# GATv2 and GCN on one core: x1 turned instead of multiplied, and six list rounds on half of the candidates

## The chip, the cores and the metric

The kernel runs on one core of one Trainium2 chip. The metric is the device time in microseconds (us) of one execution; of five executions shown for the kernel before, the median is 2499.34 us. A profiled execution gives the trace from which all durations of single instructions come. Engines are named as the profile names them: PE is TensorE (PEld its weight loads), DVE is VectorE, ACT is ScalarE, POOL is GpSimd, SP is SyncE. All data are float32.

## The reference

Two graph layers work on 3327 nodes (padded to 3328 = 26 blocks of 128) with 128 features. The adjacency matrix is dense in memory but sparse in content: a row has 63 neighbours on the average and at most 96, the node itself not counted.

```
h = relu(layernorm(x))
for each of 4 heads:
    x1, x2 = h @ w1, h @ w2
    s[i, j] = a . leaky_relu(x1[i] + x2[j])          # 128 features
    s = exp(8 tanh(s / 8)) * adj;  s = s / rowsum(s)
    out = leaky_relu(s @ h @ Wlin.T)
x = x + concat(out of the heads) @ w
h = relu(layernorm(x))
x = x + relu(D^-1/2 (adj + I) D^-1/2 (h @ W.T + b))
```

## The kernel before, in words

The kernel computes the first layer's scores only where the adjacency matrix is not zero. For this it makes, for each block of 128 rows (destinations), lists of the neighbours of each row, and gathers the neighbours' rows from a table in DRAM. A row of this table holds h, the linear part of the scores, x2 of the four heads and two stretches of adjacency weights.

A block has two halves of 64 rows, and each half is worked off in nine groups m. Groups 0 to 7 belong to the 64 list slots of each row: a gather brings 128 table rows, 8 destinations with 16 slots each. POOL issues these gathers at L595, 8 to a tile `g`, with four such tiles (`rows_in`). Group 8 is the overflow: rows with more than 64 neighbours put the rest into a shared list of up to 256 entries for each half (`oi`, `ge`, `FOUND` = 2), with up to 40 entries for one row (`EXTRA`). If a row or a half has more, a flag opens a dense path at the end of the program (`_dense_layer0`, `_dense_layer1`).

For each group, `stage_z` transposes the x2 part of the gathered rows on PE into a PSUM tile `z` (L622), two heads at a time; DVE then takes the maximum of z and x1n, which is -x1 with features on the partitions, into `r` (L638). Group 8 has a matmul of its own that adds x1 by rows, `x1b`, through a selection matrix `oi` (L625 and L627), and DVE (L633) and ACT (L635) make `r` from it. `stage_r` multiplies `r` with the attention vector (L657). `finish` takes the scores through tanh and exp and sums the weighted neighbours on PE (L706, L724). `close` finishes the block.

The lists of block b + 1 are made while block b is worked off, by the generator `prep`. At each `yield` it hands back control. `slot()` is called twice for each pair of heads of a group, some 108 times a block, and lets `prep` go on so that its 72 steps (`NPREP`) keep pace; `tails` and `ends`, the later stages of `finish` and `close`, are advanced in the same place. The order of instructions on each engine is fixed by this when the program is built.

The steps of `prep` that matter here are these:

- Rows of the adjacency matrix become codes: 0 for no edge, and otherwise the number of columns minus the column (L410). 64 segments of 52 codes each give their 8 largest with one MAX8 (L422), 32 segments for each half of the columns. The candidates of half c that the list rounds look at stand in `cand[:, c, :SOME]`, 136 values: the four largest of each segment, and the 8 largest of what is left of the half (L425).
- `select(r)` is one list round (L450 to L457): MAX8 takes the 8 largest candidates into the list (L453), and MATCH_REPLACE8 puts zeros in their places (L456). There are 13 rounds, r = 0 to 12; the last has no MATCH_REPLACE8. Rounds 0 to 7 fill the 64 slots, rounds 8 to 12 the 40 entries beyond. Which candidates a round looks at is chosen in L452: in turns one half (136 values) for r < 4, and both halves (`flat`, 272 values) from then on.
- The lists become indices (L463 to L475) and overflow entries (L486 to L547).
- x1 is computed twice from hTb, the block's h with features on the partitions. L551 makes x1 by rows with one matmul of 512 columns; ACT copies it from PSUM into `x1b` (L553). After one `yield`, L557 makes x1 with features on the partitions, with four matmuls of 128 columns, one for each head; ACT writes its negative into `x1n` (L559). Each of the two results has a bank of the PSUM pool `ps_tr`.

## Time and profile before

| | us |
|---|---|
| median of five executions | 2499.34 (2495.57 to 2508.67) |
| profiled execution | 2499.25 |
| its span, first to last instruction | 2497.5 |
| from one block's L551 to the next (671.07 to 758.63) | 87.6 |
| PE waits (PE and PEld) for DVE's L638, whole run | 114.3 and 171.2 |
| DVE waits for PE's L622 (before L638) and L627 (before L633) | 127.3 and 134.1 |
| ACT's copy into x1b (L553), mean | 0.585 |
| ACT's copy into x1n (L559), mean | 0.597 |

In a line of groups, the columns are: source line, engine, operation, what it writes and reads by the program's names, partitions x elements, count, then busy time in us and the mean of one in ns, and last the idle time of the engine just before these instructions and what ended it. A line of the timeline has the start in us, the duration in us (of a run of like instructions merged), engine, source line, operation and, in brackets, the idle time before it and who ended it. A float32 matmul stands in the profile as two passes, each with a weight load.

### The profile page before, as it was taken

Reading aid. Unit: us, or ns where it says so; the run is one execution under the profiler, and the core shown is the slowest. Engines: PE = TensorE matmul, PEld = TensorE weight load, DVE = VectorE, ACT = ScalarE, POOL = GpSimd, SP = SyncE. Lnnn points to the kernel's source line nnn. Section 1 sums busy time; section 2 is a strip of 40 time slices with the busy share of each in tenths; the row PEclk is TensorE's granted clock in tenths of the full one; section 3 lists DMA queues with packets and bytes.
Section 4 is the critical chain, followed back from the end, with each engine's and each line's share of the span. In section 5 each row is a group of like instructions: output and inputs, shape, how many; then the busy total and the mean of one; then the engine's idle time right before and its main releaser. Section 6 shows DMA issues by size and latency. Waiting matters only on the chain.

```text
span 2497.5 us, 52385 instructions
## 1 busy us (share of the span) xinstructions
PE 2255.3 (90%) x19410; PEld 1596.2 (64%) x19410; DVE 2063.2 (83%) x6426; ACT 680.9 (27%) x1703; POOL 1736.2 (70%) x1822
## 2 busy tenths in 40 slices
PE   6589999989988999999999999999999999999988
PEld 4466666666666666666676666666677666666643
DVE  7688888888898898889888888988988898896623
ACT  4122232223222222322222222232232223222110
POOL 3577777777777777777777777777777777777700
PEclk9699999999999999999999999999999999999989
DMA  9999999999999999999999999999999999999995
GB/s 299 383 337 327 357 326 323 339 349 317 335 366 321 330 351 347 323 331 364 327 327 349 337 314 334 348 321 335 351 332 321 348 352 313 335 327 348 365 273 161
DMA packets 417844, 826.94 MB, mean 331 GB/s; under 512 B 38435, under 2 KB 288815, under 8 KB 414255
## 3 DMA queue, kind: packets, MB, share of 16 engines
q0 software_dynamic: 141440, 619.41, 70.7%
q1 hardware_dynamic: 165343, 147.87, 18.5%
q10 hardware_dynamic: 110800, 56.25, 7.5%
q8 instruction: 156, 2.56, 0.4%
q14 instruction: 105, 0.86, 0.1%
HBM read 754.47 MB, written 113.22 MB: 347 GB/s over the span
## 4 chain that ended last, share of the span: by engine, by line
PE 39%; DVE 26%; DMA 17%; POOL 10%; issue 6%; ACT 1%; SPq 0%; DVEq 0%; ACTq 0%; POOLq 0%
DVE r L638 14%; DMA g<-table,idx 13%; PE z L622 13%; POOL g L595 10%; PE s L657 10%; DVE cand L422 3%; PE ag L706 2%; PE z L627 2%; DVE codes L410 1%; PE z L988 1%; DVE cand L456 1%; DMA g<-AT_d 1%; DVE lists L453 1%; PE tr L675 1%; PE tr L924 1%
## 5 line engine op out<-in xcount | busy, mean ns | idle before, releaser
L595 POOL DMA_INDIRECT g<-table,idx x1664 | 1612.3, 969 | 584.5 <-issue 417.9
L638 DVE TENSOR_TENSOR r<-z,x1n 128x1024 f32<-128x1024 f32 x832 | 1009.8, 1214 | 129.6 <-PE z L622 127.3
L622 PE MATMUL z<-ident,g 128*128 128x128 f32 x6656 | 935.1, 279 | 99.1 <-DVE r L638 88.0
L622 PEld LDWEIGHTS z<-ident,g 128*128 128x128 f32 x6656 | 754.7, 143 | 260.8 <-DVE r L638 137.7
L657 PE MATMUL s<-r,sel 128*2 128x512 f32 (+1 forms) x3744 | 497.5, 584 | 8.3 <-ACT r L635 3.9
L666 ACT COPY ssb<-s 128x512 f32<-128x512 f32 x260 | 146.6, 564 | 500.8 <-PE s L657 500.0
L657 PEld LDWEIGHTS s<-r,sel 128*2 128x2 f32 x3744 | 79.8, 83 | 249.8 <-issue 188.1
L422 DVE MAX8 cand<-codes 128x8 f32<-128x52 uint16 x1664 | 217.1, 204 | 0.0
L686 ACT ACTIVATE th<-sc 128x32 f32<-128x32 f32 x260 | 58.4, 225 | 439.1 <-DVE sc L681 412.9
L706 PEld LDWEIGHTS ag<-g,wt 128*32 128x32 f32 x3328 | 99.9, 110 | 90.2 <-issue 80.5
L367 ACT COPY at<-tr 128x512 f32<-128x512 f32 (+1 forms) x175 | 97.1, 555 | 208.5 <-PE tr L365 195.6
L675 PE MATMUL tr<-ident,ssb 128*128 128x128 f32 x988 | 150.8, 273 | 1.7 <-ACT ssb L666 1.7
L633 DVE TENSOR_TENSOR r<-z,x1n 128x128 f32<-128x128 f32 x104 | 30.0, 288 | 136.7 <-PE z L627 134.1
L706 PE MATMUL ag<-g,wt 128*32 128x133 f32 x3328 | 140.6, 281 | 0.0
L453 DVE MAX8 lists<-cand 128x8 f32<-128x272 f32 (+1 forms) x338 | 133.0, 394 | 2.2
L365 PE MATMUL tr<-ident,adjb 128*128 128x128 f32 x676 | 109.0, 284 | 26.0 <-DMA adjb<-in_adj_dram 15.8
L635 ACT ACTIVATE r<-z 128x512 f32<-128x512 f32 x104 | 62.1, 597 | 246.4 <-DVE r L633 240.3
L627 PE MATMUL z<-oi,x1b 128*128 128x256 f32 x416 | 124.3, 381 | 0.0
L675 PEld LDWEIGHTS tr<-ident,ssb 128*128 128x128 f32 x988 | 118.1, 141 | 8.6 <-ACT ssb L666 2.4
L595 POOL DMA_INDIRECT ge<-table,idxo x104 | 100.8, 969 | 31.7 <-issue 16.8
L456 DVE MATCH_REPLACE8 cand<-lists,cand 128x272 f32<-128x272 f32 (+1 forms) x312 | 117.8, 378 | 0.0
L410 DVE SCALAR_TENSOR_TENSOR codes<-adjb,code 128x832 uint16<-128x832 f32 x104 | 105.2, 1014 | 13.8 <-DMA adjb<-in_adj_dram 13.8
(199 smaller groups left out, 2406.8 us busy)
## 6 DMA issues: line engine op xcount, KB each, us to landing
adjb<-in_adj_dram SPq DMA_DIRECT2D x26, 1664.0 KB
table<-AT_d SPq DMA_DIRECT2D x26, 1664.0 KB
AT_d<-at ACTq DMA_DIRECT2D x150, 256.0 KB
g<-table,idx POOLq DMA_INDIRECT x1664
table<-img SPq DMA_DIRECT2D x12, 1296.0 KB
adjb<-AT_d SPq DMA_DIRECT2D x72, 128.0 KB
g<-AT_d ACTq DMA_DIRECT2D x25, 256.0 KB
g<-AT_d SPq DMA_DIRECT2D x25, 256.0 KB
```

The lines of the kernel that those rows point to most:

```text
L410: nc.vector.scalar_tensor_tensor(codes[:, i], adjb[:, c0:c0 + part], 0.0, code[:, c0:c0 + part], op0=OP.not_equal, op1=OP.mult, accum_out= ...
L422: nc.vector.max(cand[:, c, 8:].rearrange("p (r s) -> p r s", s=32)[:, :, sgm % 32], codes.rearrange("p a b -> p (a b)")[:, sgm % 32 * SEG: ...
L453: nc.vector.max(top, of)
L456: nc.vector.match_replace(out=of, in_to_replace=top, in_values=of, imm_value=0.0)
L595: return nc.gpsimd.indirect_dma_start(out=g[:, t, lo:hi], out_offset=None, in_=tab, in_offset=bass.IndirectOffsetOnAxis(ap=at[:, t:t + 1], ...
L622: nc.tensor.matmul(z[:, i, q * P:(q + 1) * P], g[:, m % 2 * 4 + q, c0:c0 + D], ident, is_transpose=True, start=(q == 0 or m < 8), stop=(m ...
L627: nc.tensor.matmul(z[:, i, :n], k.x1b[:, h * D:(h + 1) * D], k.oi[:, hb * n:(hb + 1) * n], start=False, stop=True, skip_group_check=True)
L638: nc.vector.tensor_tensor(r.rearrange("p h (i s) -> p h i s", s=16), z.rearrange("p h (i s) -> p h i s", s=16), k.x1n[:, 2 * hp:2 * hp + 2 ...
L657: nc.tensor.matmul(k.s[32 * h:32 * h + 2, :n], sel[:, h, 31 - at:33 - at], r[h // 2][:, h % 2, :n], start=(at == 0), stop=(at == 1 or m == 8))
L666: nc.scalar.copy(ssb[:, :nk * P], s[:, :nk * P])
L675: nc.tensor.transpose(pt[:, q, :], ssb[:, q * P:(q + 1) * P], ident)
L706: nc.tensor.matmul(ag[32 * cg:32 * cg + 32, u, :WORK], wt[:, t].rearrange("p h q -> p (h q)"), g[:, t, f0:f0 + WORK], start=(w == 0 and t ...
```

## The change

Two lines of `prep` change. Rounds 4 and 5 of the lists look at one half of the candidates each, as rounds 0 to 3 do, so that of the 64 slots 24 + 24 come from the two halves and 16 from both together. And x1 with features on the partitions is no longer multiplied from w1 and hTb; it is turned on PE from `x1b`, head by head, with `ident` as the other operand. The steps, the yields, the PSUM banks and all other instructions stay.

```diff
             def select(r):
                 top = lists[:, 8 * r:8 * r + 8]
-                of = cand[:, r % 2, :SOME] if r < 4 else flat
+                of = cand[:, r % 2, :SOME] if r < 6 else flat
                 nc.vector.max(top, of)
...
             pm = bank()
             for h in range(H):
-                nc.tensor.matmul(pm[:, h * P:(h + 1) * P], w1_sb[:, h, :], hTb, start=True, stop=True)
+                nc.tensor.transpose(pm[:, h * P:(h + 1) * P], x1b[:, h * P:(h + 1) * P], ident)
```

## Prediction, made before the result was known

> **What bounds the kernel now.** I read the page's busy shares and its chain first.

> ```profile
> PE 2255.3 (90%) x19410; PEld 1596.2 (64%) x19410; DVE 2063.2 (83%) x6426; ACT 680.9 (27%) x1703; POOL 1736.2 (70%) x1822
> PE 39%; DVE 26%; DMA 17%; POOL 10%; issue 6%; ACT 1%; SPq 0%; DVEq 0%; ACTq 0%; POOLq 0%
> ```

> No engine is the bound alone: TensorE (PE) and VectorE (DVE) hand the end to each other inside each block. The waits say so: DVE waits 134.1 us for the matmuls of L627 and 127.3 us for the transposes of L622; PE and its weight loads wait 114.3 and 171.2 us for L638 on DVE. For gathered rows PE waits only 8.0 us. So the question for each edit is which engine is late where it stands. For that I priced both edits by the groups with shapes kept apart (columns: count, busy us, mean ns), and then looked in the timeline at where they fall.

> ```profile
> L453 DVE MAX8 lists<-cand 128x8 f32<-128x272 f32 x234 | 102.6, 439 | 2.2
> L456 DVE MATCH_REPLACE8 cand<-lists,cand 128x272 f32<-128x272 f32 x208 | 88.4, 425 | 0.0
> L453 DVE MAX8 lists<-cand 128x8 f32<-128x136 f32 x104 | 30.4, 293 | 0.0
> L456 DVE MATCH_REPLACE8 cand<-lists,cand 128x136 f32<-128x136 f32 x104 | 29.4, 283 | 0.0
> ```

> **Edit 1, the list rounds (L452).** Each block has 13 rounds, r = 0 to 12. Rounds 4 and 5 go from 272 to 136 candidates: one MAX8 and one MATCH_REPLACE8 each. A round gets 439 - 293 = 146 ns and 425 - 283 = 142 ns shorter, two rounds 0.58 us, 26 blocks 15.0 us of DVE. Nothing is added or moved. What lies beside them, in block 7 (DVE alone, then PE alone):

> ```profile
> 629.26 1.22 DVE L638 TENSOR_TENSOR r<-z,x1n 128x1024 f32<-128x1024 f32 x1
> 630.39 0.43 DVE L453 MAX8 lists<-cand 128x8 f32<-128x272 f32 x1
> ...
> 632.61 0.43 DVE L453 MAX8 lists<-cand 128x8 f32<-128x272 f32 x1
> ...
> 636.26 0.29 DVE L633 TENSOR_TENSOR r<-z,x1n 128x128 f32<-128x128 f32 x1 [1.46 <-PE z L627]
> ```

> ```profile
> 630.53 0.44 PE L622 MATMUL z<-ident,ge 128*128 128x128 f32 x2 [0.97 <-DVE r L638]
> ...
> 635.63 0.60 PE L627 MATMUL z<-oi,x1b 128*128 128x256 f32 x2
> ```

> The reader is to see the order. PE's last wait for DVE ends at 630.53, on the L638 that stands before round 4 (630.39). Rounds 4 (630.39) and 5 (632.61) come after it, and then DVE stands idle for 1.46 us until PE is done with L627. Between 630.53 and 636.2 PE has no gap. So 0.58 us less on DVE only makes its idle time 1.46 + 0.58 us: PE's run over the overflow group (m = 8 of the first half) hides it, and PE is what is late next. The same wait stands behind round 6 in every block from 2 to 25 (0.33 us in block 2, 1.34 to 1.80 us after). Three blocks (3, 8, 9) have another phase: there the MAX8 of round 4 is ahead of the L638 that PE waits for (276.13 against 277.75 in block 3), so 3 x 0.146 = 0.4 us may be gained. In block 1 the rounds (119.30 to 121.3) lie in DVE's 2.65 us of idle time before 123.93, at the end of PE's 4.01 us wait for a gather. In block 0 they run at 54.3 to 56.3 under the preamble's product loop on PE (to 57.9), and the first gathers wait for SP's table stores, not for the lists. The chain agrees: its pieces on rounds 4 and 5 add up to 1.7 us in the whole run, of 67 us on all rounds. I take -0.4 us; the ends are 0 and, with no cover at all, -0.58 us a block or -15.0.

> The slots of a row also get filled differently: 24 + 24 + 16 where it was 16 + 16 + 32. The gathers keep their number and size. Counted from the reference's inputs, the overflow of 64 rows is at most 241 entries (240 before) where 256 fit, and no row leaves more than 32 where 40 fit, so the dense path at the end stays shut. I cost it at 0.

> **Edit 2, x1n (L557).** Four float32 matmuls become four transposes. The row of L557 has 208 passes for 104 matmuls, two each; the rows of transposes (L675, 988 = 26 x 38) have one each. So eight passes become four, and the operand becomes x1b, which ScalarE (ACT) writes at L553. Block 7 again, all engines:

> ```profile
> 671.07 1.02 PE L551 MATMUL tr<-w_sb,hTb 128*128 128x512 f32 x2
> 671.93 0.60 PE L622 MATMUL z<-ident,g 128*128 128x128 f32 x4
> 672.13 0.59 ACT L553 COPY x1b<-tr 128x512 f32<-128x512 f32 x1 [0.77 <-PE tr L551]
> 672.26 0.97 PEld L557 LDWEIGHTS tr<-hTb,w_sb 128*128 128x128 f32 x8
> 672.37 1.06 PE L557 MATMUL tr<-hTb,w_sb 128*128 128x128 f32 x8
> 673.15 0.25 PEld L622 LDWEIGHTS z<-ident,ge 128*128 128x128 f32 x2
> 673.47 0.60 ACT L559 ACTIVATE x1n<-tr 128x512 f32<-128x512 f32 x1 [0.74 <-PE tr L557]
> ```

> Only the four transposes of L622 stand between L551 and L557. Today L557 takes the weight path from 672.26 to 673.15, 0.89 us. Four transposes take half, 0.44, as L675's four do (weight path from 668.99 to 669.43). Alone that is -0.45 us a block. But the copy of x1b ends at 672.13 + 0.59 = 672.72, that is 0.46 us after the place where the first pass now starts. **The new wait** eats the gain. A like case is in the trace: at 143.80 the transposes of L675 wait for an ACT copy that ends at 143.75; they start 0.05 us after it, and the next weight load comes 0.39 us later. So the new L557 starts at 672.77 and the next load (673.15 now) comes between 673.16 (by that row), 673.21 (0.44 later) and 673.26 (a group of four after a wait shows 0.66 us where an unbroken one shows 0.60). That is +0.01 to +0.11 us a block; I take the middle, +0.05, times 25 blocks = +1.3 us, ends +0.3 and +2.8. In blocks 1 to 25 the copy ends 0.455 to 0.457 us after L557's start, so no block differs. Block 0 is in the preamble, beside the loads.

> Queued behind the wait on PE are L622, L625 and L627 of the overflow group, for which DVE's L633 waits (3.58 us of idle time at 679.17), and PE runs without a gap from 671 to 680. So here PE time counts one for one: the chain has 13.4 us of L557, 0.89 in 15 blocks. x1n itself ends where it did: the last pass ends 0.72 us behind the copy by the like case (143.81 + 0.66 against 143.75) and 0.71 us now (672.37 + 1.06 against 672.72). ACT's queue, SP's and POOL's keep their instructions.

> [...]

> **Sum.** -0.4 + 1.3 = +0.9 us on the profiled execution's 2499.25 us (span 2497.5 and 1.75 around it): 2500.1. The median of the runs is 2499.34, the same within 0.1 us, so I take 2500. The runs spread from 2495.57 to 2508.67, and 0.3% (7.5 us) is about what a measurement of this kernel can tell from no change.

> **Rivals.**
> - *The list rounds count in full* (DVE is the bound in them): 2499.25 - 15.0 = 2484. For it: DVE is 83% busy and 26% of the chain. Against it: the 1.46 us of idle time behind them in nearly every block. Chance 0.07.
> - *The copy is in time*: PE reaches L557 later, or the wait costs less, so that edit 2 gives its 0.45 us in 25 blocks: 2499.25 - 11.3 = 2488. It needs 0.5 us more between L551 and L557; nothing in the diff gives it. Chance 0.06.
> - *The wait is paid and the passes are not saved*, the slower side: if a transpose of x1b takes two passes, as L557's matmuls do, PE starts 0.51 us later and saves nothing, and DVE's L633 waits on: 25 x 0.51 = 12.8, 2512. It decides as soon as more than half of the wait is left uncovered. Against it: every transpose of the trace has one pass. Chance 0.08.
> - *The dense path opens* (more overflow than fits): many times the time. The count above speaks against it. 0.01.

> **How the numbers follow.** No measurable change has 0.78, faster 0.07 + 0.06 = 0.13, slower 0.08 + 0.01 = 0.09. The forecast is 2500. Below, the range goes to the second rival's 2488, so that it holds 0.78 + 0.06 = 0.84 of the chance; above to 2508, the highest run shown, which covers the wait's +2.8 and a different luck with PE's clock (0.98 granted from 1200 to 1400 us, 1.00 from 800 to 1200: some 4 us in 200).

> **What would show it.** Right: MAX8 at 136 candidates 156 times, at 272 182 times, DVE busy 15 us lower, its wait for L627 before L633 some 13 us longer; L557 with 104 passes and a PE wait "ACT x1b L553" of about 0.5 us in 25 blocks; distance from block to block unchanged (87.6 us from 671.07). Wrong: a PE gap at L557 well over 0.5 us, another 0.4 us or more gone from each block, or other gather times (today 946 ns of POOL each).

## The result and the profile after

| | before | after |
|---|---|---|
| median, us | 2502.05 (2490.57 to 2510.2, 59 runs) | 2502.84 (2493.15 to 2509.21, 33 runs) |
| ratio to before | | 0.9999, 95% interval 0.9991 to 1.0007 |
| span of the profiled execution, us | 2497.5 | 2506.0 |

The change moves nothing that can be measured; 2500 had been forecast. The profiled execution of after happens to be one of the longer ones of its kernel; why it is longer is a finding of its own, told with the experiments.

The page's busy shares and the chain by engine, after:

```profile
PE 2255.1 (90%) x19306; PEld 1580.5 (63%) x19306; DVE 2046.8 (82%) x6426; ACT 683.0 (27%) x1703; POOL 1734.3 (69%) x1822
PE 35%; DVE 25%; DMA 19%; POOL 13%; issue 6%; ACT 1%; SPq 0%; DVEq 0%; ACTq 0%; POOLq 0%
```

DVE is busy 16.4 us less (2063.2 before), PE does 104 passes less, and the span gained nothing from either. The groups of the list rounds, by shape:

```profile
L453 DVE MAX8 lists<-cand 128x8 f32<-128x272 f32 x182 | 80.0, 440 | 2.0
L456 DVE MATCH_REPLACE8 cand<-lists,cand 128x272 f32<-128x272 f32 x156 | 66.3, 425 | 0.0
L453 DVE MAX8 lists<-cand 128x8 f32<-128x136 f32 x156 | 45.7, 293 | 0.0
L456 DVE MATCH_REPLACE8 cand<-lists,cand 128x136 f32<-128x136 f32 x156 | 44.2, 283 | 0.0
```

52 instructions of each kind have moved from the long form to the short one, each 142 to 147 ns shorter. Where the time went stands in the timeline of block 7, DVE alone and then PE alone:

```profile
627.86 1.22 DVE L638 TENSOR_TENSOR r<-z,x1n 128x1024 f32<-128x1024 f32 x1
628.99 0.29 DVE L453 MAX8 lists<-cand 128x8 f32<-128x136 f32 x1
...
630.93 0.29 DVE L453 MAX8 lists<-cand 128x8 f32<-128x136 f32 x1
...
634.87 0.29 DVE L633 TENSOR_TENSOR r<-z,x1n 128x128 f32<-128x128 f32 x1 [2.03 <-PE z L627]
```

```profile
629.13 0.44 PE L622 MATMUL z<-ident,ge 128*128 128x128 f32 x2 [0.97 <-DVE r L638]
...
634.23 0.60 PE L627 MATMUL z<-oi,x1b 128*128 128x256 f32 x2
```

From PE's last wait to the L633 at the end it is 634.87 - 629.13 = 5.74 us, and before 636.26 - 630.53 = 5.73. DVE arrives 0.57 us earlier and waits 0.57 us longer (2.03 for 1.46). The x1 step of the same block, all engines:

```profile
669.56 0.30 PEld L551 LDWEIGHTS tr<-w_sb,hTb 128*128 128x128 f32 x2
...
670.72 0.58 ACT L553 COPY x1b<-tr 128x512 f32<-128x512 f32 x1 [0.76 <-PE tr L551]
...
671.36 0.42 PEld L557 LDWEIGHTS tr<-ident,x1b 128*128 128x128 f32 x4 [0.48 <-ACT x1b L553]
671.36 0.66 PE L557 MATMUL tr<-ident,x1b 128*128 128x128 f32 x4 [0.24 <-ACT x1b L553]
671.75 0.25 PEld L622 LDWEIGHTS z<-ident,ge 128*128 128x128 f32 x2
...
672.06 0.60 ACT L559 ACTIVATE x1n<-tr 128x512 f32<-128x512 f32 x1 [0.75 <-PE tr L557]
```

The four transposes start 0.05 us after the copy's end, after a wait that was not there before; the weight path takes 0.42 us where the eight passes took 0.97. From L551's first weight load to the first load behind L557 it is 671.75 - 669.56 = 2.19 us; before it was 673.15 - 670.97 = 2.18. The wait eats what the passes give back, to 0.01 us.

### The profile page after: what moved, and what is told of

Same layout as the page of the kernel before. It is cut to its first block, busy times and chain, and to the rows that moved or that the text cites. A ratio compares the mean times of both kernels' runs of the same rounds, so it can differ in the third digit from the quotient of the medians.

```text
span 2506.0 us, 52175 instructions
## 1 busy us (share of the span) xinstructions
PE 2255.1 (90%) x19306; PEld 1580.5 (63%) x19306; DVE 2046.8 (82%) x6426; ACT 683.0 (27%) x1703; POOL 1734.3 (69%) x1822
## 4 chain that ended last, share of the span: by engine, by line
PE 35%; DVE 25%; DMA 19%; POOL 13%; issue 6%; ACT 1%; SPq 0%; DVEq 0%; ACTq 0%; POOLq 0%
DMA g<-table,idx 15%; DVE r L638 14%; POOL g L595 13%; PE z L622 11%; PE s L657 9%; DVE cand L422 3%; PE ag L706 2%; PE z L627 2%; PE z L988 1%; PE tr L379 1%; DMA g<-AT_d 1%; DVE codes L410 1%; DVE cand L456 1%; DVE lists L453 1%; PE tr L924 1%
## 5 line engine op out<-in xcount | busy, mean ns | idle before, releaser
L638 DVE TENSOR_TENSOR r<-z,x1n 128x1024 f32<-128x1024 f32 x832 | 1009.8, 1214 | 136.8 <-PE z L622 135.1
L622 PE MATMUL z<-ident,g 128*128 128x128 f32 x6656 | 936.2, 280 | 99.7 <-DVE r L638 88.6
L622 PEld LDWEIGHTS z<-ident,g 128*128 128x128 f32 x6656 | 755.1, 143 | 261.5 <-DVE r L638 138.3
L657 PE MATMUL s<-r,sel 128*2 128x512 f32 (+1 forms) x3744 | 504.0, 591 | 8.6 <-DVE r L638 4.1
L633 DVE TENSOR_TENSOR r<-z,x1n 128x128 f32<-128x128 f32 x104 | 30.0, 288 | 150.0 <-PE z L627 147.4
L675 PE MATMUL tr<-ident,ssb 128*128 128x128 f32 x988 | 150.8, 273 | 1.7 <-ACT ssb L666 1.7
L453 DVE MAX8 lists<-cand 128x8 f32<-128x272 f32 (+1 forms) x338 | 125.7, 372 | 2.0
L627 PE MATMUL z<-oi,x1b 128*128 128x256 f32 x416 | 124.3, 381 | 0.0
L595 POOL DMA_INDIRECT ge<-table,idxo x104 | 101.4, 975 | 32.4 <-issue 12.8
L675 PEld LDWEIGHTS tr<-ident,ssb 128*128 128x128 f32 x988 | 118.1, 141 | 8.6 <-ACT ssb L666 2.4
L456 DVE MATCH_REPLACE8 cand<-lists,cand 128x136 f32<-128x136 f32 (+1 forms) x312 | 110.5, 354 | 0.0
```

Of the source, the lines that this page charges most:

```text
L453: nc.vector.max(top, of)
L456: nc.vector.match_replace(out=of, in_to_replace=top, in_values=of, imm_value=0.0)
L595: return nc.gpsimd.indirect_dma_start(out=g[:, t, lo:hi], out_offset=None, in_=tab, in_offset=bass.IndirectOffsetOnAxis(ap=at[:, t:t + 1], ...
L622: nc.tensor.matmul(z[:, i, q * P:(q + 1) * P], g[:, m % 2 * 4 + q, c0:c0 + D], ident, is_transpose=True, start=(q == 0 or m < 8), stop=(m ...
L627: nc.tensor.matmul(z[:, i, :n], k.x1b[:, h * D:(h + 1) * D], k.oi[:, hb * n:(hb + 1) * n], start=False, stop=True, skip_group_check=True)
L638: nc.vector.tensor_tensor(r.rearrange("p h (i s) -> p h i s", s=16), z.rearrange("p h (i s) -> p h i s", s=16), k.x1n[:, 2 * hp:2 * hp + 2 ...
```

## The experiments

All ratios are against the kernel before, run beside it on the same chip, with 95% intervals; microseconds are worked out from medians.

The theory was that each edit lies where it cannot act: the list rounds under PE's overflow group, the transposes behind the copy of x1b. The rivals were that the two edits cancel, that DVE is the bound, and that POOL's gathers with the DMA set the pace whatever PE and DVE do.

**e1, the list rounds alone.** The line of L557 is put back:

```diff
-                nc.tensor.transpose(pm[:, h * P:(h + 1) * P], x1b[:, h * P:(h + 1) * P], ident)
+                nc.tensor.matmul(pm[:, h * P:(h + 1) * P], w1_sb[:, h, :], hTb, start=True, stop=True)
```

> The list rounds alone (rounds 4 and 5 on 136 candidates), x1n multiplied as before. Theory (both edits lie where they cannot act: the rounds under PE's overflow group, the turn behind a new wait): 0 us against before, at most -2; DVE busy 15 us lower, its idle time before the second L633 about 0.58 us longer in each block (1.46 to about 2.03). Rival 1 (the two edits cancel: the rounds bring what the wait costs): -5 us or more. Rival 2 (DVE is the bound): -15 us.

Measured: 2505.91 us, ratio 1.0025 (1.0013 to 1.0037). Less work on DVE, and 6 us slower: no theory had this. DVE's idle time before L633 is 2.03 us in most blocks, as expected, so the edit does locally what it should.

**e2, the transposes alone.** `r < 6` is put back to `r < 4`.

> The transposes alone, list rounds as before. Theory: 0 to +2 us against before; PE waits about 0.5 us for x1b in each block, its next weight load comes where it came before. Rival 1 (the two edits cancel): +5 us or more. Rival 3 (four passes less count whatever the wait): -11 us.

Measured: 2501.0 us, ratio 1.0002 (0.9989 to 1.0016), as the theory has it. That the two edits cancel falls here: there is no cost in this one that could take back a gain of the other, and the other one gained nothing.

**e3, the transposes one step later**, so that the copy is done when PE reaches them:

```diff
-            pm = bank()
-            for h in range(H):
-                nc.tensor.transpose(pm[:, h * P:(h + 1) * P], x1b[:, h * P:(h + 1) * P], ident)
-            x1n = pb.tile([P, H, P], F32, name="x1n")
-            nc.scalar.activation(x1n, pm[:, :H * P].rearrange("p (h i) -> p h i", h=H), AF.Copy, scale=-1.0)
             pmx = pb.tile([P, 16, H], F32, name="pmx", bufs=1)
             nc.vector.tensor_tensor(pmx, tmask[:, :, None].to_broadcast([P, 16, H]),
                                     p_all[:, b, None, :H].to_broadcast([P, 16, H]), OP.mult)
             yield
+            pm = bank()
+            for h in range(H):
+                nc.tensor.transpose(pm[:, h * P:(h + 1) * P], x1b[:, h * P:(h + 1) * P], ident)
+            x1n = pb.tile([P, H, P], F32, name="x1n")
+            nc.scalar.activation(x1n, pm[:, :H * P].rearrange("p (h i) -> p h i", h=H), AF.Copy, scale=-1.0)
             yield
```

> The changed kernel with the four transposes and the ACT copy to x1n one step of prep later, behind pmx, so that x1b is ready when PE gets there. Theory: the wait of 0.5 us goes and the four passes saved, 0.45 us, show in the blocks where PE sets the end there (15 to 25 of 26): -7 to -11 us against before. Rival 4 (POOL's gathers and the DMA set the pace and no edit on PE or DVE shows): 0 us. It could be spoiled if PE then has a gap in another place of the same stretch.

Measured: 2491.73 us, ratio 0.9966 (0.9952 to 0.998), -8.6 us. PE and its weight loads in block 7 of this kernel:

```profile
665.42 0.60 PE L622 MATMUL z<-ident,g 128*128 128x128 f32 x4
665.96 0.20 PEld L622 LDWEIGHTS z<-ident,ge 128*128 128x128 f32 x2 [0.18 <-DVE r L638]
...
666.78 0.60 PE L561 MATMUL tr<-ident,x1b 128*128 128x128 f32 x4
```

The transposes (L561 here) follow without a wait. Of the 0.45 us saved, 0.18 goes to a new wait: PE now comes to the overflow group before DVE has freed its bank. The rest, 0.27 us in 25 blocks, is 6.8 us; 8.6 was measured, within the interval. So PE time counts in this stretch, and POOL with the DMA does not set the pace there.

**e4, two more MAX8 in round 5**, into a tile that nobody reads:

```diff
                 nc.vector.max(top, of)
+                if r == 5:
+                    for _ in range(2):
+                        nc.vector.max(pb.tile([P, 8], F32, name="spare"), flat)
                 yield
```

> The changed kernel with two more MAX8 over 272 candidates in round 5, into a tile that nobody reads: 2 x 0.44 = 0.88 us of DVE more in each block, 23 us in all. Theory: the idle time before the second L633 (2.03 us) takes them, 0 us against before, at most +2, and that idle time falls to about 1.15 us. Rival 2 (DVE is the bound in these rounds): +23 us. Rival 4: 0 us too, so this run does not tell it apart.

Measured: 2507.39 us, ratio 1.003 (1.0016 to 1.0044), +7 us. The 23 us of the rival did not come, and the idle time before L633 fell from 2.03 to 1.34 us in most blocks, so that it took up nearly all of the two MAX8 (0.77 us together in the timeline of block 7); but +7 is more than the theory allows. So e1 took work away and e4 added some, both at a place with idle time to spare, and both came out slower.

**What e1 and e4 have in common.** I set the blocks' lengths, from one L551 to the next (the one that begins with block n's L551 is called n here, and holds rounds 4 and 5 of block n + 1), beside the stretches in which the profile shows PE's granted clock at half (0.50). In blocks 2 to 24 these last 3.41 us each. In the kernel before, nine of them lie there, and a block with one is longer. Lengths of three blocks in us, a star where a half-clock stretch lies in the block:

| kernel | block 6 | block 10 | block 20 | half-clock stretches in blocks 2 to 24 | of them 38 to 41 us behind L551 |
|---|---|---|---|---|---|
| before | 86.8 | 87.0 | 87.8 | 9 | 6 |
| after | 86.8 | 88.5* | 87.8 | 14 | 13 |
| e1 | 86.8 | 88.5* | 87.8 | 12 | 11 |
| e2 | 86.8 | 87.0 | 87.8 | 4 | 2 |
| e3 | 86.5 | 86.7 | 87.5 | 6 | 5 |
| e4 | 88.4* | 87.1 | 87.8 | 11 | 7 |

Without a star, before, after, e1, e2 and e4 have the same length to 0.1 us in these three blocks; e3 alone is shorter, by 0.3. So neither edit has a cost or a gain of its own in them. A stretch costs some 1.5 to 1.6 us (88.5 for 87.0 us in block 10, 88.4 for 86.8 in block 6). Most of them come about 39 us behind L551. What stands ahead of them is, in the windows of the kernel after (block 10; columns: window, its length, busy us of PE, PEld, DVE, ACT and POOL, PE's clock, DMA share, GB/s):

```profile
966.60:970.00 3.40, 3.40 (x45) 2.86 (x38) 3.40 (x17) 0.96 (x2) 1.63 (x2) 1.00 1.08 398
970.00:973.40 3.40, 1.61 (x14) 1.13 (x12) 3.33 (x15) 2.55 (x3) 2.48 (x4) 1.00 1.03 353
973.50:976.90 3.40, 3.40 (x20) 1.44 (x22) 3.37 (x10) 0.77 (x2) 2.49 (x4) 0.50 0.96 319
```

```profile
973.22 1.72 PE L622 MATMUL z<-ident,g 128*128 128x128 f32 x8 [1.61 <-DVE r L638]
```

PE is busy for 1.61 of 3.40 us in the window ahead, since it waits 1.61 us for DVE behind the second MAX8 of L425, in every block from 2 to 24; the next window has half the clock. In the kernel before the same gap stands in the same blocks, with the half clock in some. The nine half-clock stretches in blocks 2 to 24 of before start a whole number of 3.4133 us apart, to 0.003 us, and so do the 14 of after; I divide each trace into windows of that length, in step with its stretches. In the profile of before the gap lies whole in one such window in 11 blocks: the six windows with PE busy for 1.55 to 1.62 us are followed by half the clock, the five with 1.67 to 1.81 us are not. In the profile of after it does so in 15 blocks, and half the clock follows in 13 (1.61 to 1.73 us, not with 1.74 and 1.80). Where the gap falls across two windows, in 12 and 8 blocks, it follows in none. So at this gap the half clock came only where the whole gap lay in one window, and PE was not idle in that window: it was busy for nearly half of it, 1.55 to 1.73 of 3.41 us.

**e5 to e8, the gap filled.** Theory 2 from here on: the spread of the runs, and the 6 to 7 us of e1 and e4, come from such windows. PE gets something to do in the gap:

```diff
                     nc.vector.max(cand[:, c, :8], cand[:, c, SOME:])
+                    if c == 1 and b:
+                        nc.tensor.matmul(bank(), ident, w1_sb.rearrange("p h d -> p (h d)"), start=True, stop=True)
```

e5 is the changed kernel with it, e6 the kernel before, e7 the late transposes of e3, and e8 the changed kernel with a cut in two later rounds (it leaves out of the lists what these rounds miss, and the dense path that would make up for it). Its other edits beside the matmul are

```diff
-                of = cand[:, r % 2, :SOME] if r < 6 else flat
+                of = cand[:, r % 2, :SOME] if r < 6 or r in (10, 11) else flat
...
-            nc.vector.tensor_reduce(flag, flags, AX.X, OP.add)
+            nc.vector.memset(flag, 0.0)
```

> The changed kernel with one matmul of 512 columns into a bank that nobody reads (two passes, 0.86 us of PE) put behind the second MAX8 of L425 in each block from 1 on. It lies in the 1.61 us in which PE waits for DVE there (36.8 to 38.4 us behind the block's L551). Theory 2, on what spreads the runs: a clock window of 3.41 us with PE busy for only about half of it (1.70 of 3.50 us) is followed by one at half clock, which makes a block some 1.7 us longer; with the gap filled the half-clock windows about 39 us behind L551 (10 to 12 in the profile of the changed kernel) go: -15 to -20 us against before, and the runs lie closer together. Rival 5 (the half clock has nothing to do with this gap): 0 us, or up to +10 if the matmul delays what is behind it.

> The kernel before with the same matmul in the gap. Theory 2: -12 to -18 us against before, and within 2 us of the changed kernel with the matmul, since both edits of the change act on nothing. Rival 6 (the change itself brings or costs some us that the clock hid): the two filled kernels differ by 5 us or more.

> The matmul in the gap and the transposes one step later, the two together. Theory: the gain of the late transposes (0.3 to 0.45 us a block, 7 to 11 us) on top of the filled kernel: -22 to -31 us against before. Rival 5: -8 us, as the late transposes alone.

> The changed kernel with the matmul in the gap, and rounds 10 and 11 too on one half of the candidates each; what these two rounds miss is left out of the lists, and the flag that would open the dense path is set to zero. The cut is 0.58 us a block, as that of rounds 4 and 5, but in a stretch where the chain runs over these rounds (MAX8 10 and 11 and MATCH_REPLACE8 10 have some 10 us each on it). Theory: about 0.43 us of it count in 23 blocks, -10 us against the filled kernel. Rival 4 (POOL and DMA set the pace) and the reading that the list rounds are nowhere on the path: 0 against the filled kernel.

Measured: before 3408.38 us beside them; e5 1.0087 (1.0058 to 1.0117), e6 0.9999 (0.9977 to 1.0021), e7 1.0038 (1.0014 to 1.0063), e8 1.006 (1.0034 to 1.0087). The same kernel before takes 36% longer here, on a chip that bears the same number as the one of e9 to e12, and the matmul did not help there: e6 is no faster, and the other three are slower. These four are not evidence on the kernel at 2500 us for either side, since the chain is another one too; that of e6 is:

```profile
PE 54%; DVE 15%; another core or an unknown queue 12%; issue 10%; DMA 5%; POOL 2%; ACT 1%; ACTq 0%; SPq 0%; DVEq 0%; POOLq 0%
```

For 12% of the time something outside the core's known queues is the releaser (10% in e5, e7 and e8), which no profile at 2500 us has. What it was stays open. Three of the four kernels were run again; the kernel before with the matmul (e6) was not, so its time at 2500 us is not known.

**e9, the gap filled** (the kernel of e5).

> The kernel of e5 again (the changed kernel with one unread matmul of 512 columns in PE's 1.61 us gap behind L425), since the chip of e5 to e8 ran the kernel before at 3408 us and its profile is another one. Theory 2 (a 3.41 us window with PE busy for half of it is followed by one at half clock): the half-clock windows some 39 us behind L551 go from blocks 1 to 24, -15 to -20 us against before. Rival 5 (the gap and the half clock have nothing to do with each other): 0 to +10 us.

Measured: 2493.17 us against 2501.83, ratio 0.996 (0.9944 to 0.9975), -8.7 us. PE and the windows of block 10 (L624 is L622 here, L427 the new matmul):

```profile
961.59 1.02 PE L427 MATMUL tr<-w_sb,ident 128*128 128x512 f32 x2
962.45 1.47 PE L624 MATMUL z<-ident,g 128*128 128x128 f32 x12
965.08 1.09 PE L624 MATMUL z<-ident,g 128*128 128x128 f32 x8 [1.16 <-DVE r L640]
```

```profile
963.00:966.40 3.40, 2.24 (x21) 1.65 (x23) 3.37 (x13) 3.13 (x3) 2.48 (x4) 1.00 1.02 382
966.40:969.80 3.40, 3.40 (x45) 2.17 (x38) 3.21 (x10) 0.59 (x1) 2.63 (x3) 1.00 0.98 311
```

The gap shrinks to 1.16 us; a stretch of 3.40 us laid over it has PE busy for 2.24 us, and the clock stays full. In this block the gap falls across two of the windows that are in step with the half-clock stretches of e9; in the 13 blocks of e9 where it lies whole in one, PE is busy there for 2.19 to 2.39 us, and the full clock follows in all 13. No half-clock stretch is left near 39 us behind L551 in blocks 2 to 24; three are left in them, at 16 and 29 us, where PE has other gaps (2.0 us ahead of L379; 0.7 and 1.0 us ahead of L748 and L624). Blocks without a star keep 86.8, 87.0 and 87.8 us, so the matmul itself costs nothing. The size was expected too high (-15 to -20): the profile of after, with 14 stretches, was one of its longer executions.

**e10, the list rounds alone with the gap filled** (e1 with the matmul).

> The list rounds alone (as e1, which ran +6 us) with the same matmul in the gap. Theory 2 (e1 lost its 6 us to the clock alone, and the list rounds act on nothing): within 2 us of the filled changed kernel. Rival 6 (shorter list rounds cost or bring time of their own): it stays 5 us or more away from the filled changed kernel.

Measured: 2493.41 us, ratio 0.9962 (0.9949 to 0.9976), 0.2 us from e9. With the gap filled, e1 and the changed kernel take the same time. These two differ in the transposes alone, so this confirms that the transposes act on nothing. That the list rounds act on nothing in most blocks is shown by the lengths of those without a star: 86.8, 87.0 and 87.8 us for blocks 6, 10 and 20 in e10 and e9, as in before.

**e11, the gap filled and the transposes late** (the kernel of e7).

> The matmul in the gap and the transposes one step later. Theory: the late transposes' 0.3 us a block (86.5 and 87.5 us against 86.8 and 87.8 in blocks without a half-clock window, 7 to 8 us in all) on top of the filled kernel: -22 to -28 us against before. Rival 5: -8 us, as the late transposes alone.

Measured: 2484.38 us, ratio 0.9929 (0.9916 to 0.9943), -17.5 us, which is 8.8 us below e9: the late transposes bring here what they brought alone. The six runs lie within 3.6 us (2482.92 to 2486.49), the twelve of before beside them within 9.4; but e9's six lie within 7.9 and e10's seven within 8.3, so the filled gap alone does not end the spread. This is the version that beats both kernels and computes all of the reference.

**e12, the same cut of the list rounds at another place** (the kernel of e8).

> The filled changed kernel with rounds 10 and 11 too on one half of the candidates; what these rounds miss is left out of the lists, and the flag that would open the dense path is set to zero. The same cut of 0.58 us a block as that of rounds 4 and 5, in a stretch where the chain runs over them. Theory (the place decides): about 0.43 us of it count in 23 blocks, -10 us against the filled changed kernel. Rival 4 (POOL and the DMA set the pace): 0 us against the filled changed kernel.

Measured: 2481.04 us, ratio 0.9915 (0.99 to 0.993), 12.1 us below e9. DVE in block 7 of e9, and then of e12 (L455 is the MAX8 of round 11, L640 is L638):

```profile
644.89 0.45 DVE L455 MAX8 lists<-cand 128x8 f32<-128x272 f32 x1
...
651.84 1.23 DVE L640 TENSOR_TENSOR r<-z,x1n 128x1024 f32<-128x1024 f32 x1 [1.07 <-PE z L624]
```

```profile
641.29 0.28 DVE L455 MAX8 lists<-cand 128x8 f32<-128x136 f32 x1
...
648.08 1.22 DVE L640 TENSOR_TENSOR r<-z,x1n 128x1024 f32<-128x1024 f32 x1 [1.18 <-PE z L624]
```

In this stretch L638 runs back to back with the rounds, and DVE's next wait grows by 0.11 us only, where behind rounds 4 and 5 it grew by all of 0.57. The same 0.58 us cut at rounds 10 and 11 is worth 0.4 to 0.6 us a block (blocks 6, 10 and 20: 86.4, 86.5 and 87.3).

## Why the prediction was right

- *No engine is the bound alone; the place decides.* Shown: e3 (PE) and e12 (DVE) each gain, at places where that engine is late, what the change saved in vain.
- *Edit 1, -0.4 us of 15.0, the rest hidden by PE's overflow group.* Shown: DVE's waits for L627 rose from 134.1 to 147.4 us in the whole run, by 13.3 of the 16.4 us that DVE is busy less, and blocks without a half-clock stretch kept their length, but for a few. The three blocks of another phase gave more than the -0.4: the stretches that hold their rounds (2, 7 and 8 in the count of the table) are 0.2 to 0.4 us shorter each in e9 and e10 than in e2, which has the long rounds; so the 87.6 us from 671.07, expected to stay, became 87.3 (669.66 to 756.96), and the term should have been about -1 us. The clock nearly hid all this: e1 by itself would have refuted it at +6 us. That after, with the same rounds, came out at +0.8 us is therefore in part luck.
- *Edit 2, +0.01 to +0.11 us a block.* Shown: 2.19 for 2.18 us, the lower end, e2 at 1.0002, and e10 equal to e9. The like case it was taken from, L675 waiting for ACT's copy, fits to 0.01 us. x1n ends where it did: 3.00 us behind L551's matmul in both (673.47 + 0.60 - 671.07; 672.06 + 0.60 - 669.66).
- *The rival "the copy is in time", 11.3 us.* e3 made its condition true and got 8.6: the step missed was that DVE is late next there, by 0.18 us a block.
- *The list rounds count in full* and *the passes are not saved*: refuted by the blocks of e1 (86.8 us in block 6, as before, and not 86.2), and by the 104 passes, four of them in 0.42 us.
- *The transposes and PE's clock.* That the transposes lower it is not shown: e2, with the transposes alone, has four half-clock stretches in blocks 2 to 24, before nine. These are one profile each, and the granted clock differs from run to run (0.975 to 0.983 in e2, 0.976 to 0.983 in before), but its mean agrees: 0.9787 in 12 runs of e2, 0.9789 in 35 of before beside them.
- *What the range's upper end put down to PE's clock*, some 4 us in 200, named a cause of the spread that the runs bear out: inside each of before, e1 and e4, 0.001 more of mean granted clock goes with 1.3 to 1.9 us less (straight lines through their runs). What the prediction did not see is that many of the half-clock stretches sit on one gap that repeats in blocks 2 to 24.

Open: e1 and e4 do run at a lower clock, a mean of 0.9764 in 12 runs each for 0.9789 in the 35 of before beside them; by those slopes that makes some 3 to 5 of their 6 and 7 us. What the rest is stays open. Not all of it sits on the gap: in the profile of e4, 6.8 us of its extra time lie behind the last block's L551 (248.4 us at clock 0.94 for 241.6 at 0.96). Open too is why the clock is lower with the short rounds (0.9767 in the 35 runs of after as well, but 0.9782 in e3, which has them too), and why after, at the clock of e1, was not slower than the kernel before beside it.

## What to carry to other kernels

Price a cut at the next wait behind it on the same engine: if that engine already stands idle there, the cut only lengthens the idle time (2.03 for 1.46 us here), and the same cut at another place can count (0.4 to 0.6 us a block in e12, of the 0.58 taken out). An operand that another engine has just made can bring a wait with it (0.48 us for PE here, none one step later in e3); look how long ago that copy ended where the instruction stands, and move the instruction rather than the operand. Where runs spread by several microseconds, find what the spread is made of before reading a difference of that size as an effect of an edit.
